# One pool of eight PSUM banks and no root tables in a two-layer kernel; squares on ScalarE; the gate, the weighted sums and the factors of operands on GpSimd

## The chip, the core and the metric

The kernel runs on one core of a Trainium2 chip. The core has a matrix engine (TensorE, PE in the profile; its weight loads are PEld), three engines for elementwise work (VectorE or DVE, ScalarE or ACT, GpSimd or POOL), a queue that issues DMAs (SP), a memory for tiles of 128 partitions (SBUF), and an accumulator memory, PSUM, of eight banks of 128 x 512 float32, which TensorE fills and VectorE and ScalarE read. The metric is the device time of one launch in microseconds (us). Everything is float32.

## The reference

Two transformer layers over x of shape 16 x 512 x 128 (sequences b = 0..15, 512 tokens, width 128), each an attention and a feed-forward part on the same normalised input:

```python
# layer 0
xn = layernorm(x)
q, k = phi(rope(xn @ Wq.T)), phi(rope(xn @ Wk.T))        # 16 heads of 8; phi = elu + 1
num, den = cumulative sums over earlier tokens of k v and of k, applied to q
attn = (num / max(den, 1e-6)) @ Wo.T
p, i = top_k(softmax(xn @ router_w.T), 2)                # of 8 experts
moe = sum over the two: p / sum(p) * square(relu(xn @ w_fc[e].T)) @ w_proj[e].T
x = x + attn + moe + square(relu(xn @ shared_fc.T)) @ shared_proj.T
# layer 1
xn = layernorm(x)
# softmax attention in chunks of 64 queries, each chunk seeing the keys up to its own end;
# each head's probabilities are scaled by a gate computed from their sum (two steps of a small
# dynamical system with tanh, clips and products), then normalised again
attn = out @ W_out.T
mix = sigmoid(xr @ W_r.T) * (square(relu(xk @ W_k.T)) @ W_v.T)   # xr, xk blend xn with the token before
x = x + attn + mix
```

## The kernel before

**Tiling.** A sequence is four tiles of 128 tokens. The 16 sequences go in groups of 3, 4, 4, 3 and 2 (`GROUPS`, L47). For a group, `dispatch` (L1042) normalises x, routes the tokens and scatters them to expert slots in DRAM by indirect DMAs from POOL (`send`, L1091). `slot_tiles` (L1126) goes over the slot tiles four at a time: SP fetches rows and each tile's expert weights, `hidden` (L1168) makes the hidden activations of a pair of tiles (product, relu on ScalarE, square on VectorE or POOL, L1181), `project` (L1184) the second product, and results go back to DRAM. `layer0` runs the linear attention of each sequence (`linear_operands` L831, `linear_attention` L921) and then `shared_expert` (L1010). `layer1` runs for each sequence a `head` (L1526: gather both experts' rows and add them, `combine` L1219; layernorm; `channel_mix` L1451; values; `projected` L1298; `operands` L1307) and a `body` (L1546) of two halves u = 0 and 1, each of eight heads; `tail` (L1482) applies the gate (`gated` L1427, `gate_factor` L1237) and the output product.

**Layer 1's attention.** `operands` first computes score units (sc) for the row maxima: five units for each half, each of 4 x 512 columns in strips of 32 rows, which VectorE reduces (maxima). `weighted` (L1365) computes the scores again with the maxima folded in (st), takes the exponential on ScalarE (ex) and accumulates the products with v into `po` (o1, L1369), which stays open for the whole half. Factors for operands: for u = 0 VectorE makes qa and ka in one instruction each, for u = 1 POOL makes each in two (L1317 to 1322).

**PSUM.** Two pools: `ps_big` with three tiles of two banks and `ps_one` with two tiles of one bank (L509 to 516). Scores (sc, st) take two big tiles for a unit; hg, h, qkv, qk and the transposes of q and k take a big one; all others take one of the two single banks.

**Order.** The program is not written in the order of issue. Generators emit operations with their engine and data needs; `Program.run` (L332) is a planner that walks a simulated clock with a cost for each kind of instruction (`COSTS`, L215; `TURN`, L222, for PE's change between full-height and 32-row or 32-column products) and picks for each engine the earliest operation that is ready; buffers are handed out in simulated time too (`_take`, L414). What it picks becomes the fixed order on each engine. Operations inside `with program.unit()` (L326) stay together on PE. An indirect DMA is "spaced" (L472): it waits for the PE instruction that was emitted last before it (L474), and at least 1.9 us of simulated time lie between two. All engine instructions come out of one helper, so the profile gives them all as L261; groups are told apart by the tiles they write and read. L1095 and L1114 are the indirect DMAs.

**Layernorm** (L649): statistics on VectorE, the root on ScalarE (L657), which shares that engine with exponentials and tanh, reciprocal and normalisation on VectorE.

## Time and profile before

| | |
|---|---|
| median of the runs | 1670.35 us (1669.26 to 1676.13, 3 runs) |
| profiled execution | 1665.29 us, of which the span from first to last instruction 1663.5 us |
| instructions | 36439 |
| mean granted clock of TensorE | 0.973 |
| indirect DMAs on POOL | 128 scatters of 1.06 us, 128 gathers of 1.00 us |
| ACT table loads | 48 of 1.28 us |
| reductions for the maxima | 448, 385.8 us on VectorE |
| DMA | 167.03 MB, 99 GB/s to and from HBM over the span |

A busy PE in the profile is not PE at its peak: the ends of products are modelled, and a product that stands waiting inside a run of products counts as busy. In the table by stage a stretch of the span is a line: its length, the busy time of each engine with the number of instructions, TensorE's granted clock, the share of DMA time. In groups, what follows the first bar is busy us and the mean ns of one instruction; what follows the second is the idle time just before them and who ended it. A line of waits gives the total, how often, and the longest.

### The profile page before, as it was taken

To read this page: it belongs to the slowest core of one execution; us is meant where nothing else is said; L and a number is where in the kernel's file an instruction comes from. 1 tells how busy PE (TensorE), PEld (TensorE's weight loads), DVE (VectorE), ACT (ScalarE), POOL (GpSimd) and SP (SyncE) were. 2 spreads that over 40 slices of the span, in tenths; PEclk is the share of its full clock that TensorE was granted. 3 is DMA by queue.
4 is the path that set the end of the run, shared out by engine and by line. 5 is a ranking of instruction groups with operands and counts; after the bars stand their busy time and mean duration, and the time that the engine had idled before them with its cause. 6 is when DMAs were issued, how large, how long until landed. Compare 5 with 4: busy or idle time off the path is not lost.

```text
span 1663.5 us, 36439 instructions
## 1 busy us (share of the span) xinstructions
PE 1547.3 (93%) x14439; PEld 1021.8 (61%) x14439; DVE 1207.5 (73%) x2474; ACT 778.2 (47%) x1191; POOL 539.1 (32%) x485
## 2 busy tenths in 40 slices
PE   4889799999999999999999989999999999999996
PEld 3578776666766566566666656666565656565443
DVE  7875268877578874976758796968786858786773
ACT  4343334545445634444544655454545444535444
POOL 1415255075125421453033603242136202135020
PEclk8899999999999999999999999999999999999998
DMA  5367777144334423243322243324133313110000
GB/s 155 106 211 233 219 218 212 49 141 118 96 107 127 127 87 96 72 121 97 90 90 79 78 122 96 96 63 124 35 94 92 110 33 86 30 51 23 20 1 14
DMA packets 154986, 167.03 MB, mean 100 GB/s; under 512 B 13248, under 2 KB 100672, under 8 KB 154816
## 3 DMA queue, kind: packets, MB, share of 16 engines
q1 hardware_dynamic: 146624, 147.91, 29.9%
q0 software_dynamic: 8192, 16.79, 3.3%
q8 instruction: 114, 1.87, 0.5%
q14 instruction: 56, 0.46, 0.1%
HBM read 122.83 MB, written 41.81 MB: 99 GB/s over the span
## 4 chain that ended last, share of the span: by engine, by line
PE 53%; DVE 10%; issue 5%; ACT 3%; POOL 1%; DMA 0%; SPq 0%; POOLq 0%; ACTq 0%; DVEq 0%
PE o L261 10%; PE sc L261 10%; PE st L261 8%; PE yg_ps L261 5%; PE hg_ps L261 5%; DVE maxima L261 4%; PE y L261 3%; PE h_ps L261 2%; PE qkv L261 1%; PE qk L261 1%; PE ho_a L261 1%; ACT ex L261 1%; PE oh_a L261 1%; PE mx L261 1%; PE cm_r L261 1%
## 5 line engine op out<-in xcount | busy, mean ns | idle before, releaser
L261 DVE TENSOR_REDUCE maxima<-sc 128x2 f32<-128x768 f32 (+2 forms) x448 | 385.8, 912 | 84.6 <-PE sc L261 83.0
L261 ACT ACTIVATE ex<-st 128x1024 f32<-128x1024 f32 x320 | 313.1, 1025 | 177.5 <-PE st L261 176.3
L261 PE MATMUL st<-qa,ka 32*128 32x384 f32 (+3 forms) x2048 | 213.4, 471 | 9.6 <-DVE maxima L261 5.9
L261 PE MATMUL sc<-ka,qa 32*128 32x512 f32 (+2 forms) x1792 | 213.8, 511 | 3.7 <-DVE maxima L261 1.0
L1095 POOL DMA_INDIRECT rows<-xn,pl_slot x128 | 135.1, 1055 | 225.6 <-PE y L261 64.2
L261 PE MATMUL yg_ps<-wp,hg 128*128 128x128 f32 x1304 | 188.5, 287 | 17.5 <-DVE hg L261 9.4
L261 PEld LDWEIGHTS yg_ps<-wp,hg 128*128 128x128 f32 x1304 | 162.6, 195 | 66.9 <-issue 36.6
L1114 POOL DMA_INDIRECT back<-results,pl_slot x128 | 128.4, 1003 | 222.7 <-PE st L261 38.4
L261 PE MATMUL hg_ps<-xgT,wf 128*128 128x128 f32 x1304 | 182.5, 285 | 10.8 <-issue 6.3
L261 DVE TENSOR_TENSOR am<-sc,const_sb 128x1024 f32<-128x1024 f32 x128 | 151.3, 1218 | 53.7 <-PE sc L261 49.2
L261 PEld LDWEIGHTS hg_ps<-xgT,wf 128*128 128x128 f32 x1304 | 163.5, 196 | 35.9 <-issue 23.8
L261 PE MATMUL o<-ex,vpad 128*32 128x512 f32 (+3 forms) x2048 | 175.1, 447 | 1.7 <-ACT yg L261 1.3
L261 PEld LDWEIGHTS st<-qa,ka 32*128 32x128 f32 x2048 | 104.0, 186 | 81.4 <-issue 26.4
L261 ACT ACTIVATE hg<-hg_ps 128x1024 f32<-128x1024 f32 x84 | 84.2, 1002 | 135.7 <-PE hg_ps L261 135.3
L261 POOL TENSOR_TENSOR hg<-hg 128x1024 f32<-128x1024 f32 x34 | 64.6, 1901 | 224.1 <-ACT hg L261 223.9
L261 PEld LDWEIGHTS sc<-ka,qa 32*128 32x128 f32 x1792 | 90.5, 185 | 70.5 <-issue 25.8
L261 PEld LDWEIGHTS o<-ex,vpad 128*32 128x32 f32 x2048 | 52.2, 110 | 83.8 <-issue 59.5
L261 DVE TENSOR_TENSOR hg<-hg 128x1024 f32<-128x1024 f32 (+1 forms) x50 | 62.0, 1241 | 56.4 <-ACT hg L261 56.4
L261 ACT COPY oTs<-o 128x256 f32<-128x256 f32 (+1 forms) x96 | 42.7, 445 | 120.2 <-PE o L261 119.5
L261 ACT COPY yg<-yg_ps 128x256 f32<-128x256 f32 x84 | 30.9, 368 | 131.6 <-PE yg_ps L261 108.6
L261 PE MATMUL o<-am,vpad 128*32 128x128 f32 x2048 | 81.8, 281 | 8.7 <-DVE am L261 8.0
L261 PE MATMUL sc<-q0m,k0T 32*128 32x256 f32 x1024 | 81.3, 410 | 1.6 <-ACT ex L261 1.0
(193 smaller groups left out, 2289.1 us busy)
## 6 DMA issues: line engine op xcount, KB each, us to landing
wf<-in_w_fc SPq DMA_DIRECT2D x163, 256.0 KB
wp<-in_w_proj SPq DMA_DIRECT2D x163, 256.0 KB
results<-yg SPq DMA_DIRECT2D x79, 128.0 KB
xg<-rows SPq DMA_DIRECT2D x37, 256.0 KB
rows<-zeros SPq DMA_DIRECT2D x2, 2496.0 KB
x_in<-in_x SPq DMA_DIRECT2D x16, 256.0 KB
x<-x SPq DMA_DIRECT2D x16, 256.0 KB
out<-rr SPq DMA_DIRECT2D x16, 256.0 KB
```

What stands on the lines that cost most here:

```text
L261: return getattr(api, method)(*map(made, args), **{k: made(a) for k, a in kw.items()})
L1095: i = nc.gpsimd.indirect_dma_start(out=rows.made()[:, :], out_offset=bass.IndirectOffsetOnAxis(ap=slot.made(), axis=0), in_=row.made(), in ...
L1114: "POOL", lambda: nc.gpsimd.indirect_dma_start(out=o.made(), out_offset=None, in_=results.made()[:, :], in_offset=bass.IndirectOffsetOnAxi ...
```

## The change

- **PSUM**: one tile of eight banks (`Banks`). A tile asks for one bank or for two adjacent ones; the planner picks which, by the earliest time and by how many banks it would leave without their neighbour. hg and h take single banks, one relu each, as do the transposes of q and of k.
- **Root**: POOL adds the epsilon and takes the power -0.5; the Sqrt on ScalarE and VectorE's reciprocal are gone.
- **Squares**: those that VectorE made (hg and h) are a Square on ScalarE; those on POOL stay, and so does channel_mix's.
- **To POOL**: the gate's arithmetic but for reciprocals and fused operations; the weighted sum of expert rows (one product with the share, one add, for all four tiles); the masked copies of q in layer 0 (q0m, before on ScalarE from PSUM); the operands of u = 1 in wider instructions; for the last two sequences (`LATE`) also the operands of u = 0, the normalisation and the gate's factor.
- **To ScalarE**: the two scalings in channel_mix.
- **Units**: the products of a hidden tile, of `project`, of `projected` and of `shared_expert`'s y stay together on PE.
- **Planner**: costs for POOL and for scalar operands of VectorE changed; two small routing tiles share buffers with others.

```diff
+LATE = B - GROUPS[-1]
...
+class Banks:
+    def __init__(self, pool, n, ahead):
+        self.pool, self.n, self.whole = pool, n, None
+        self.slots = Slots(n, ahead)
+        self.slots.free = [(0.0, k) for k in range(n)]
+    def tile(self, shape, name):
+        base = Base(self.slots, lambda: self._made(base))
+        base.psum, base.banks = True, shape[1] if len(shape) == 3 else 1
+        self.slots.asked.append(base)
+        base.turn = len(self.slots.asked) - 1
+        return View(base, shape)
+    def _made(self, base):
+        if self.whole is None:
+            self.whole = self.pool.tile([P, self.n, 512], F32, tag="banks", name="banks")
+        if base.banks == 1:
+            return self.whole[:, base.at[0], :]
+        return self.whole[:, base.at[0] : base.at[0] + base.banks, :]
+    @staticmethod
+    def place(slots, bs, start):
...
-    ("ACT", None): (200, 0.8), ("POOL", None): (120, 1.75), ("SP", None): (80, 0.0),
+    ("ACT", None): (200, 0.8), ("POOL", None): (240, 1.63), ("POOL", "fast"): (120, 1.14),
+    ("POOL", "each"): (60, 2.97), ("POOL", "memset"): (100, 0.84), ("SP", None): (80, 0.0),
 }
+EACH = 75
...
-    ps_big = pool("ps_big", 3, 24, space=bass.MemoryType.PSUM)
-    ps_one = pool("ps_one", 2, 24, space=bass.MemoryType.PSUM)
+    banks = Banks(
+        ctx.enter_context(tc.tile_pool(name="psum", bufs=1, space=bass.MemoryType.PSUM)), 8, 48
+    )
     def big(name):
-        return ps_big.tile([P, 2, 512], F32, tag="big", name=name)
+        return banks.tile([P, 2, 512], name)
     def one(name):
-        return ps_one.tile([P, 512], F32, tag="one", name=name)
+        return banks.tile([P, 512], name)
...
-    eps = fixed.tile([P, 1], F32, tag="eps", name="eps")
-    V.memset(eps, LN_EPS)
+    root = fixed.tile([P, NT], F32, tag="root", name="root")
+    V.memset(root, -0.5)
...
-    def layernorm_T(xs, xT, name, tag, bufs):
+    def layernorm_T(xs, xT, name, tag, bufs, late=False):
...
-        S.activation(rstd, mv[:, :, 1], AF.Sqrt, bias=eps, scale=1.0)
-        V.reciprocal(rstd, rstd)
+        G.tensor_scalar_add(rstd, mv[:, :, 1], LN_EPS)
+        G.tensor_tensor(rstd, rstd, root, ALU.pow)
         xn = p2.tile([P, NT, D], F32, tag=tag, name=f"xn_{name}", bufs=bufs)
         for t in range(NT):
-            V.tensor_scalar(
+            (G if late else V).tensor_scalar(
...
-        pts = big(f"qkT_ps_{b}")
-        for s in range(2):
+        q_tag, k_tag, bufs = home["T"]
+        both = []
+        for s, (tag, n) in enumerate(((q_tag, "q0T"), (k_tag, "k0T"))):
+            pts = one(f"qkT_ps_{b}_{s}")
             for t in range(NT):
                 M.transpose(
-                    pts[:, s, t * P : (t + 1) * P], qr[:, t, s * D : (s + 1) * D], ident
+                    pts[:, t * P : (t + 1) * P], qr[:, t, s * D : (s + 1) * D], ident
                 )
-        q_tag, k_tag, bufs = home["T"]
-        qT = p2.tile([P, T], F32, tag=q_tag, name=f"q0T_{b}", bufs=bufs)
-        S.copy(qT, pts[:, 0, :])
-        kT = p2.tile([P, T], F32, tag=k_tag, name=f"k0T_{b}", bufs=bufs)
-        S.copy(kT, pts[:, 1, :])
+            oT = p2.tile([P, T], F32, tag=tag, name=f"{n}_{b}", bufs=bufs)
+            S.copy(oT, pts)
+            both.append(oT)
+        qT, kT = both
         qms = []
         for u in range(2):
             tag, bufs = home["q0m"]
             qm = (p3 if tag == "probs" else p2).tile(
                 [P, 2, T], F32, tag=tag, name=f"q0m_{b}_{u}", bufs=bufs
             )
-            for o in range(2):
-                r = 2 * u + o
-                S.activation(qm[:, o, :], pts[:, 0, :], AF.Copy, scale=c_("pick")[:, r : r + 1])
+            G.tensor_tensor(
+                qm, qT.unsqueeze(1).to_broadcast([P, 2, T]),
+                c_("pick")[:, 2 * u : 2 * u + 2].unsqueeze(2).to_broadcast([P, 2, T]), ALU.mult,
+            )
...
         for fp in range(2):
-            ph = big(f"h_ps_{b}_{fp}")
+            hf = hs[fp]
             for i in range(2):
                 f = 2 * fp + i
-                M.matmul(
-                    ph[:, i, :], wfc_s[:, f * P : (f + 1) * P], xnT, start=True, stop=True
-                )
-            hf = hs[fp]
-            S.activation(hf, ph, AF.Relu)
-            (V if fp or b < GROUPS[0] else G).tensor_tensor(hf, hf, hf, ALU.mult)
+                ph = one(f"h_ps_{b}_{f}")
+                M.matmul(ph, wfc_s[:, f * P : (f + 1) * P], xnT, start=True, stop=True)
+                S.activation(hf[:, i, :], ph, AF.Relu)
+            if fp or b < GROUPS[0]:
+                S.activation(hf, hf, AF.Square)
+            else:
+                G.tensor_tensor(hf, hf, hf, ALU.mult)
...
+        with program.unit():
+            for t in range(NT):
+                cols = slice(t * P, (t + 1) * P)
+                M.matmul(py[:, t, :], oT[:, cols], w_("wo0"), start=True, stop=False)
...
         def hidden(xgT, ws, q, pair):
-            ph = big(f"hg_ps_{g}_{q}_{pair}")
+            h = p2.tile([P, 2, FF], F32, tag="hid", name=f"hg_{g}_{q}_{pair}", bufs=4)
+            o = h[:, 0 : len(ws), :]
             for ii, (wf, _) in enumerate(ws):
                 i = 2 * pair + ii
-                for f in range(NF):
-                    M.matmul(
-                        ph[:, ii, f * P : (f + 1) * P], wf[:, f * P : (f + 1) * P],
-                        xgT[:, i * P : (i + 1) * P], start=True, stop=True,
-                    )
-            h = p2.tile([P, 2, FF], F32, tag="hid", name=f"hg_{g}_{q}_{pair}", bufs=4)
-            o = h[:, 0 : len(ws), :]
-            S.activation(o, ph[:, 0 : len(ws), :], AF.Relu)
-            (V if pair or g == 0 else G).tensor_tensor(o, o, o, ALU.mult)
+                ph = one(f"hg_ps_{g}_{q}_{i}")
+                with program.unit():
+                    for f in range(NF):
+                        M.matmul(
+                            ph[:, f * P : (f + 1) * P], wf[:, f * P : (f + 1) * P],
+                            xgT[:, i * P : (i + 1) * P], start=True, stop=True,
+                        )
+                S.activation(h[:, ii, :], ph, AF.Relu)
+            if pair or g == 0:
+                S.activation(o, o, AF.Square)
+            else:
+                G.tensor_tensor(o, o, o, ALU.mult)
             return h
         def project(h, ws, n):
             py = one(f"yg_ps_{g}_{n}")
-            for ii, (_, wp) in enumerate(ws):
-                for f in range(NF):
-                    M.matmul(
-                        py[:, ii * P : (ii + 1) * P], h[:, ii, f * P : (f + 1) * P],
-                        wp[:, f, :], start=(f == 0), stop=(f == NF - 1),
-                    )
+            with program.unit():
+                for ii, (_, wp) in enumerate(ws):
+                    for f in range(NF):
+                        M.matmul(
+                            py[:, ii * P : (ii + 1) * P], h[:, ii, f * P : (f + 1) * P],
+                            wp[:, f, :], start=(f == 0), stop=(f == NF - 1),
+                        )
...
-            for t in range(NT):
-                n = k * NT + t
-                V.scalar_tensor_tensor(
-                    x1[:, t, :], y[:, t, :], shares[j][:, n, :], x1[:, t, :],
-                    ALU.mult, ALU.add,
-                )
+            share = shares[j][:, k * NT : (k + 1) * NT, :]
+            G.tensor_tensor(y, y, share.to_broadcast([P, NT, D]), ALU.mult)
+            G.tensor_tensor(x1, x1, y, ALU.add)
...
         n = NT * H
+        A = G
         def new(tag):
             return tiny.tile([P, n], F32, tag=f"gf_{tag}", name=f"gf_{tag}_{b}", bufs=1)
         rl, en, sc, cur, v, w, z, g = (new(x) for x in ("rl", "en", "sc", "cur", "v", "w", "z", "g"))
         V.reciprocal(rl, sums)
-        V.tensor_mul(en, sums, rl)
-        V.tensor_scalar_max(sc, en, 1e-6)
+        A.tensor_mul(en, sums, rl)
+        A.tensor_scalar_max(sc, en, 1e-6)
         V.reciprocal(cur, sc)
-        V.tensor_mul(cur, cur, en)
+        A.tensor_mul(cur, cur, en)
         S.activation(g, en, AF.Tanh, bias=gate_bias, scale=5.0)
-        V.tensor_scalar(g, g, 0.45, 0.55, ALU.mult, ALU.add)
-        V.tensor_mul(cur, cur, g)
...
+        A.tensor_mul(rl, rl, g)
+        A.tensor_mul(rl, rl, z)
...
-        def spread(name, k):
-            a = c_(name)[:, k * HALVES : (k + 1) * HALVES]
-            return a.unsqueeze(2).to_broadcast([P, HALVES, P // 2])
+        def spread(name, k, n):
+            a = c_(name)[:, k * HALVES : (k + n) * HALVES]
+            return a.unsqueeze(2).to_broadcast([P, n * HALVES, P // 2])
         at_ = PAIR if u == 0 else 0
-        def build(o, i, own, aug):
-            if u == 0:
-                V.scalar_tensor_tensor(halves(o), halves(i), own, aug, ALU.mult, ALU.add)
-            else:
-                G.tensor_scalar_mul(o, i, own)
-                G.tensor_tensor(halves(o), halves(o), aug, ALU.add)
+        q, k = qk[:, 0, :], qk[:, 1, :]
+        own = c_("own")[:, u : u + 1]
+        parity = c_("parity")[:, 2 * u : 2 * u + 2]
         qa = p2.tile([P, T], F32, tag="qa", name=f"qa_{b}_{u}")
-        build(qa, qk[:, 0, :], c_("own")[:, u : u + 1], spread("aug_q", u))
         ka = p2.tile([P, 2, T], F32, tag="ka", name=f"ka_{b}_{u}")
-        for k in range(2 * u, 2 * u + 2):
-            build(
-                ka[:, k % 2, :], qk[:, 1, :], c_("parity")[:, k : k + 1], spread("aug_k", k)
+        if u == 0 and b < LATE:
+            V.scalar_tensor_tensor(
+                halves(qa), halves(q), own, spread("aug_q", u, 1), ALU.mult, ALU.add
             )
+            for o in range(2):
+                V.scalar_tensor_tensor(
+                    halves(ka[:, o, :]), halves(k), parity[:, o : o + 1],
+                    spread("aug_k", 2 * u + o, 1), ALU.mult, ALU.add,
+                )
+        else:
+            G.tensor_tensor(qa, q, own.to_broadcast([P, T]), ALU.mult)
+            G.tensor_tensor(halves(qa), halves(qa), spread("aug_q", u, 1), ALU.add)
+            G.tensor_tensor(
+                ka, k.unsqueeze(1).to_broadcast([P, 2, T]),
+                parity.unsqueeze(2).to_broadcast([P, 2, T]), ALU.mult,
+            )
+            ka_ = ka.rearrange("p o t -> p (o t)")
+            G.tensor_tensor(halves(ka_), halves(ka_), spread("aug_k", 2 * u, 2), ALU.add)
...
-        V.tensor_tensor(ov, ov, fac.unsqueeze(2).to_broadcast([P, NT * H, DH]), ALU.mult)
+        (G if b >= LATE else V).tensor_tensor(ov, ov, fac.unsqueeze(2).to_broadcast([P, NT * H, DH]), ALU.mult)
...
-            V.tensor_scalar_mul(m, xp[:, 0:T], om)
+            S.activation(m, xp[:, 0:T], AF.Copy, scale=om)
...
-        yield from layernorm_T(x1, xp[:, 1 : T + 1], f"1_{b}", "xn1", 1)
+        yield from layernorm_T(x1, xp[:, 1 : T + 1], f"1_{b}", "xn1", 1, b >= LATE)
```

## The prediction

> **What bounds the kernel.** I read, in this order: busy time by engine, a table by stage, the timeline of two stretches, TensorE's waits, the groups. First, the engines:
>
> ```profile
> PE 1547.3 (93%) x14439; PEld 1021.8 (61%) x14439; DVE 1207.5 (73%) x2474; ACT 778.2 (47%) x1191; POOL 539.1 (32%) x485
> ```
>
> TensorE (PE) looks like the bound, with 1663.5 - 1547.3 = 116 us idle. The busy figure hides more. Timeline near the end (start, duration, engine, group):
>
> ```profile
> 1594.12 1.14 PE L261 MATMUL sc<-ka,qa 32*128 32x512 f32 x8
> ...
> 1600.88 7.16 DVE L261 TENSOR_REDUCE maxima<-sc 128x2 f32<-128x768 f32 x10
> ...
> 1601.44 6.65 PE L261 MATMUL sc<-ka,qa 32*128 32x384 f32 x32
> ```
>
> One score unit (all of it 2048 result columns in four strips) takes 1.14 us. The last line is two units, so 2.3 us of work "busy" for 6.65 us: PE sits inside a unit until VectorE (DVE) has reduced a PSUM tile and freed it. Over the whole span the groups give 213.8 + 81.3 us for 224 units of sc (1.32 each) and 213.4 us for 160 of st (1.33): 0.19 us above 1.14, times 384 units, is **73 us of stall hidden in "busy"**. Stages, with busy us of PE, PEld, DVE, ACT, POOL, then clock, DMA share, GB/s:
>
> ```profile
> 0.00:40.00 40.00, 19.29 (x72) 12.46 (x73) 29.44 (x116) 17.73 (x34) 7.97 (x24) 0.90 0.53 161
> 160.00:240.00 80.00, 70.40 (x599) 63.86 (x597) 31.91 (x54) 28.18 (x45) 32.95 (x29) 0.95 0.69 211
> 240.00:280.00 40.00, 37.25 (x287) 27.57 (x287) 39.27 (x87) 15.43 (x27) 23.51 (x20) 0.96 0.62 189
> 520.00:560.00 40.00, 40.00 (x416) 25.20 (x408) 35.69 (x96) 27.66 (x38) 17.42 (x18) 1.00 0.31 96
> 560.00:600.00 40.00, 34.89 (x262) 23.31 (x257) 35.43 (x73) 20.74 (x35) 18.71 (x17) 0.91 0.51 149
> 960.00:1000.00 40.00, 34.98 (x279) 21.95 (x281) 37.72 (x81) 20.28 (x31) 4.85 (x3) 1.00 0.36 104
> ```
>
> A good stretch keeps PE full. Where it falls to 35, DVE stands at 35 to 39 of 40: there DVE sets the pace. At 160 to 240 (experts of group 0) DVE is idle more than half, and PE waits on latency. The mean clock of 0.973 is worth 0.027 x 1663.5 = 45 us; the first two slices of 40 us (0.90, 0.84) and the last (0.72 over 23.5) hold 17 of it, the rest follows idle stretches in the body. So PE is the bound, with some 190 us of stall and 28 us of clock around it. PE's waits (total, times, longest):
>
> ```profile
> PE y L261 <- ACT oT_a L261: 1.3, 2, 0.7
> ...
> PE o L261 <- ACT yg L261: 1.3, 1, 1.3
> ```
>
> Both are a product waiting for the evacuation of an unrelated tile: both tiles live in the two single banks (L515), and o1 (L1369) keeps one of these for a whole half of an attention. Such lines add to about **20 us**.
>
> **The change, part by part.** Groups that price it (busy, mean ns, idle before):
>
> ```profile
> L261 POOL TENSOR_TENSOR hg<-hg 128x1024 f32<-128x1024 f32 x34 | 64.6, 1901 | 224.1 <-ACT hg L261 223.9
> ...
> L261 DVE TENSOR_TENSOR hg<-hg 128x1024 f32<-128x1024 f32 (+1 forms) x50 | 62.0, 1241 | 56.4 <-ACT hg L261 56.4
> ...
> L261 ACT ACT_TABLE_LOAD x48 | 61.6, 1283 | 21.2 <-PE st L261 19.2 <-PEq L1699 0.7 <-DVE phi L261 0.6
> ...
> L261 DVE SCALAR_TENSOR_TENSOR x<-back,rt_m,x 128x128 f32<-128x128 f32 x128 | 45.1, 404 | 10.6 <-DMA back<-results,pl_slot 10.6
> ```
>
> *DVE* loses the squares (62.0 + 23.0 us), 20 small operations of the gate for each of 16 batches (their rows add to 80.1), the weighted sums (45.1), the scaling in channel_mix (9.4 + 7.7), the reciprocal of layernorm (5.4), and for the last two batches some 10 (operands 4.9, normalising 3.9, factor 1.4): **-243 us, to about 965**. The 386 us of maxima stay.
>
> *ScalarE* gains 69 squares at 1.02 us (ex, the same 128x1024, has 1025 ns; +71), 84 + 32 relus as two of 0.60 instead of one of 1.02 (+19), 32 scalings at 0.71 (q0m, a copy with a scale per partition, has 713 ns; +23); it loses 47 of 48 table loads (-60), q0m (39.4 busy), roots (-10): +4 in all, hidden under its 885 us of idle. Here a rule weighs otherwise. The row: 1.28 us for a load, 21.2 us of idle before all 48. The Trainium skill (ScalarE: Activation LUTs, "What ACT_TABLE_LOAD costs") adds a drain of about 1.38, so the loads would be worth 47 x 2.66 = 125 us. The row shows at most 0.44 us before each, so I take 60; by the rule ScalarE would end 65 us lower and the sum below would move only where it waits for ScalarE at the start, by perhaps 5.
>
> *GpSimd (POOL)* takes the gate: 11 two-tensor operations of 64 columns (1901 at 1024 and 1059 at 512 columns give 217 + 1.64 n, so 0.32 us) and 9 with a scalar (0.18 to 0.3): 5.4 us for a batch, against 5.0 on DVE, **+87**; the sums, 32 x 2 x 1.06 = +68; q0m, 32 x 1.90 = +61; operands of the second half as 1.06 + 1.06 + 1.90 + 1.90 = 6 us instead of 8, -32; late work +19; the root's add and power, unseen: between 0.2 (two of the shortest, memset 0.105) and 2.1 us (two as long as an indirect DMA's 1.05); I take 0.6, near the small operations, +19. Together **539 to about 760**. The second rule speaks against this. The skill (SBUF — State Buffer, "Who interferes with whom") says that DVE instructions with two SBUF inputs or in a two-port mode share a port pair with GpSimd under an exclusive lock. The trace has it:
>
> ```profile
> 962.92 1.89 POOL L261 TENSOR_TENSOR h<-h 128x1024 f32<-128x1024 f32 x1 [11.77 <-ACT h L261]
> 974.36 1.89 POOL L261 TENSOR_TENSOR hg<-hg 128x1024 f32<-128x1024 f32 x1 [9.54 <-ACT hg L261]
> ```
>
> and DVE's 64-column gf_z at 974.40 lasts 1.94 us, not 0.23. Summed over DVE's instructions against their own undisturbed time the loss is 55 us. GpSimd's arithmetic grows from about 265 to 490 us, by which the rule alone would make it 102. But DVE's instructions of that kind (squares 85, gate 80, normalising 48, sums 45, rotation and phi 74, operands 39, mixing 44, others 15) fall from about 430 us to 200, so 55 x 1.85 x 0.465 = 47: no worse. By the rule alone DVE would gain 55 us less, and the sum some 10 less.
>
> *Waits that it adds.* The sum of a batch waits in POOL's queue for four gathers to land; behind it stand the next gathers and scatters, each tied to a position of PE (L474), and behind those q0m (awaited by the scores of layer 0), the gate and the second half's operands. q0m is ready at 0.59 + 3.8 us after the transposes instead of 0.59 + 0.60 + 2.44, +0.8 us, hidden by the other chains' products (DVE and PE of layer 1). SP gets no new DMA, but a store of x1 or out comes later with its sum. If the cover goes, 0.8 x 16 = 13 us.
>
> *PSUM.* One pool lets hg and h take single banks freed one by one, and leaves the pairs to the scores.
>
> *The sum*, with the ends of what can't be seen:
> - score units: 73 us of stall, 0 (the reductions alone pace it) to 73; a third, since reductions stay: 24
> - PE idle in slices where DVE is full (240, 560, 680, 960, 1040, 1280: 21 us): half, 10
> - single banks: 20 us, half, 10
> - experts of group 0: 9.6 us idle, half; the square follows two relus of which one overlaps products: 5
> - start: five table loads of 1.28 lie between roots and exponentials there; 4 of 6.4
> - changes of form: of 410 stretches of full-height work, 91 hold only a projection, only a y or only an hg; units bring some together: 50 x 0.15 us (L222 reckons 138 to 208 ns) = 8, between 0 and 20
> - clock: 6 of 28
> - against it: the last batch's gate, alone at the end (8.3 us of PE idle), on two engines with some ten handovers: -3; both halves' operands of the last batch in one queue: -2; lateness in POOL's queue, 0.4 us for a batch: -6 (0 to 25).
>
> 67 - 11 = 56. The profiled execution took 1665.3 us, so 1609; the median shown is 5 above it: **1614 us** (3.4% less).
>
> **Rivals.**
> *PE's order is the bound* and stays so: reductions pace the scores, idle DVE time goes nowhere. For it: PE is full at 520 to 560 with DVE at 35.7. Then only start and single banks: 14 - 11, so **1667**, the change not doing what it says. Against it: the slices where DVE is full.
> *The score stalls go altogether*: the 49 us not counted, and a little clock: **1560**. Against it: ten reductions at 0.72 us each in the 7.16 above.
> *GpSimd's queue becomes the bound*, the slower one. Each batch hands over there four times (gather and sum, q0m, gate, operands); gathers wait for PE and block the rest. For it: POOL waits up to 20.4 us at a gather for PE. Against it: POOL idles 1124 us. Decisive at 56/16 = 3.5 us for a batch uncovered; at 5.5 us the loss is 88: +32, **1702**.
>
> **How the numbers follow.** Forecast 0.56 (its own range 1590 to 1640), PE's order 0.10, all stalls gone 0.14, queue 0.20. Under 0.5% a measurement can't tell a change from none (1662 to 1679). Faster: 0.56 + 0.14 + half of the second = 0.75; same 0.05; slower 0.20. The range leaves out half of the third case below and about half of the queue's above: 1565 to 1690.
>
> **What would show it.** DVE near 965 us and no slice above 36 of 40; one table load; POOL near 760; sc and st near 1.25 us for a unit; fewer waits for unrelated evacuations; the gap before the last oh_a at 10 to 11 us. I am wrong if sc and st stay at 1.32, or if PE waits for POOL (q0m, ka, xn) by more than some 20 us in all; a square that needs its own table would show as loads again.

## The result, and the profile after

The changed kernel takes **1727.1 us** (median of 4 runs, 1721.1 to 1733.1) where the kernel before took 1672.7 beside it: ratio **1.0325**, 95% interval 1.028 to 1.037. It is slower by 54 us; the forecast was 1614, and its range ended at 1690. The profiled execution took 1721.1 us, its span is 1718.7.

The engines' sums came out roughly as reckoned. Busy time of the changed kernel, and from its groups the one table load that is left:

```profile
PE 1524.8 (89%) x14439; PEld 1011.4 (59%) x14439; DVE 1023.7 (60%) x1877; ACT 783.6 (46%) x1260; POOL 796.6 (46%) x951
```
```profile
L317 ACT ACT_TABLE_LOAD x1 | 1.3, 1283 | 0.7 <-PEq L1791 0.7
```

VectorE (DVE) lost 184 us, ScalarE gained 5, GpSimd (POOL) gained 258. TensorE (PE) is busy 22 us less, but its idle time went from 116 to 194 us, and its granted clock from 0.973 to 0.960: one minus the clock, times the span, is 45 us before and 69 after. Where PE waits (total, times, longest), first in the kernel before, then in the changed one, where every PSUM tile is called banks:

```profile
PE ln_ps L261 <- DVE xn L261: 11.4, 2, 9.4
...
PE oh_a L261 <- DVE o1n L261: 8.3, 1, 8.3
...
PE st L261 <- DVE maxima L261: 5.9, 11, 1.5
```

```profile
PE banks L317 <- DVE maxima L317: 39.5, 43, 5.4
PE banks L317 <- DVE xn L317: 28.2, 6, 9.3
...
PE banks L317 <- POOL o1n L317: 11.3, 1, 11.3
...
PE banks L317 <- POOL hg L317: 9.5, 5, 3.5
...
PE banks L317 <- POOL xk L317: 5.8, 5, 2.7
...
PE banks L317 <- POOL q0m L317: 2.0, 2, 1.1
...
PE banks L317 <- POOL xn L317: 1.3, 3, 0.4
```

All such lines together, PE's waits for VectorE went from 74 to 109 us, those for ScalarE from 22 to 44, those for GpSimd itself from under 1 to 30. The largest growth of single kinds is in the waits for VectorE's reductions (10.5 to 39.5, all tiles together) and for normalised rows (11.4 to 28.2). The score units as groups (busy, mean ns of one, idle before), before and then after:

```profile
L261 PE MATMUL st<-qa,ka 32*128 32x384 f32 (+3 forms) x2048 | 213.4, 471 | 9.6 <-DVE maxima L261 5.9
L261 PE MATMUL sc<-ka,qa 32*128 32x512 f32 (+2 forms) x1792 | 213.8, 511 | 3.7 <-DVE maxima L261 1.0
...
L261 PE MATMUL sc<-q0m,k0T 32*128 32x256 f32 x1024 | 81.3, 410 | 1.6 <-ACT ex L261 1.0
```
```profile
L317 PE MATMUL banks<-ka,qa 32*128 32x512 f32 (+2 forms) x1792 | 195.7, 517 | 33.3 <-DVE maxima L317 15.9
L317 PE MATMUL banks<-qa,ka 32*128 32x512 f32 (+3 forms) x2048 | 197.9, 473 | 18.7 <-DVE maxima L317 10.6
...
L317 PE MATMUL banks<-q0m,k0T 32*128 32x256 f32 x1024 | 79.7, 419 | 8.3 <-DVE maxima L317 5.8
```

A unit of sc takes (195.7 + 79.7) / 224 = 1.23 us, one of st 1.24, as forecast. But the stall only stepped out of the unit and stands in front of it: busy and idle together were 508.5 + 14.9 = 523 us before and are 473.3 + 60.3 = 534 now. Three stretches of 40 us (columns as in the table by stage of before):

```profile
240.00:280.00 40.00, 29.16 (x194) 22.87 (x194) 18.29 (x43) 10.92 (x18) 24.54 (x25) 0.83 0.40 121
...
560.00:600.00 40.00, 30.79 (x306) 19.28 (x304) 23.02 (x63) 16.46 (x24) 25.39 (x27) 0.83 0.38 112
...
960.00:1000.00 40.00, 35.41 (x353) 22.18 (x345) 29.23 (x56) 19.36 (x31) 31.05 (x33) 0.96 0.37 107
```

PE is far from full although VectorE stands at only 18 to 29 of 40. All three lie where the expert results of a group of batches are gathered. The whole stretch of gathers of the second group, of before and then of after:

```profile
499.00:602.00 103.00, 96.89 (x895) 62.57 (x897) 88.70 (x210) 57.70 (x84) 48.57 (x46) 0.97 0.39 115
```
```profile
528.00:654.00 126.00, 109.96 (x990) 73.09 (x992) 78.36 (x147) 54.63 (x88) 85.75 (x95) 0.93 0.40 119
```

GpSimd is busy 68% of it instead of 47%, and that leaves out what it waits; over the whole span it is 46%. Its queue there (start, duration, and in brackets the idle time before and its releaser):

```profile
544.36 1.04 POOL L1193 DMA_INDIRECT back<-results,pl_slot  x1 [1.90 <-PE banks L317]
545.42 0.33 POOL L317 TENSOR_TENSOR gf_rl<-gf_rl,gf_z 128x64 f32<-128x64 f32 x1
547.13 1.04 POOL L317 TENSOR_TENSOR back<-back,rt_m 128x512 f32<-128x512 f32 x1 [1.37 <-DMA back<-results,pl_slot]
548.25 1.27 POOL L317 TENSOR_TENSOR x<-x,back 128x512 f32<-128x512 f32 x1
549.67 0.99 POOL L1193 DMA_INDIRECT back<-results,pl_slot  x1
550.96 0.94 POOL L1193 DMA_INDIRECT back<-results,pl_slot  x1 [0.31 <-issue]
552.83 0.94 POOL L1193 DMA_INDIRECT back<-results,pl_slot  x1 [0.93 <-PE banks L317]
554.08 0.94 POOL L1193 DMA_INDIRECT back<-results,pl_slot  x1 [0.30 <-issue]
558.94 1.04 POOL L317 TENSOR_TENSOR back<-back,rt_m 128x512 f32<-128x512 f32 x1 [3.92 <-DMA back<-results,pl_slot]
560.06 1.26 POOL L317 TENSOR_TENSOR x<-x,back 128x512 f32<-128x512 f32 x1
561.47 0.99 POOL L1193 DMA_INDIRECT back<-results,pl_slot  x1
```

Four gathers, then the product, which stands 3.92 us until the last gather has landed, then the addition, and only then the next gather. In the kernel before, the gathers run on while VectorE adds beside them (lines between these are left out):

```profile
508.31 0.95 POOL L1114 DMA_INDIRECT back<-results,pl_slot  x1 [1.11 <-PE hg_ps L261]
...
509.58 1.13 DVE L261 SCALAR_TENSOR_TENSOR x<-back,rt_m,x 128x128 f32<-128x128 f32 x4
...
510.25 1.02 POOL L1114 DMA_INDIRECT back<-results,pl_slot  x1 [1.00 <-PE hg_ps L261]
...
512.39 0.94 POOL L1114 DMA_INDIRECT back<-results,pl_slot  x1 [1.11 <-PE hg_ps L261]
```

### The profile page after: what moved, and what is told of

The parts are those of the page before. It is cut to its first block, busy times and chain, and to the rows that moved or that the text cites. A ratio compares the mean times of both kernels' runs of the same rounds, so it can differ in the third digit from the quotient of the medians.

```text
span 1718.7 us, 36520 instructions
## 1 busy us (share of the span) xinstructions
PE 1524.8 (89%) x14439; PEld 1011.4 (59%) x14439; DVE 1023.7 (60%) x1877; ACT 783.6 (46%) x1260; POOL 796.6 (46%) x951
## 4 chain that ended last, share of the span: by engine, by line
PE 64%; DVE 15%; POOL 8%; issue 5%; DMA 4%; ACT 4%; POOLq 0%; SPq 0%; DVEq 0%; ACTq 0%
PE banks L317 64%; DVE maxima L317 5%; DMA back<-results,pl_slot 3%; POOL back L1193 1%; ACT ex L317 1%; DVE am L317 1%; POOL back L317 1%; DVE xn L317 1%; ACT hg L317 1%; POOL ln_rstd L317 1%; DVE qr L317 1%; POOL gf_z L317 1%; DVE pl_ef L317 1%; POOL x L317 1%; POOL rows L1174 1%
## 5 line engine op out<-in xcount | busy, mean ns | idle before, releaser
L317 DVE TENSOR_REDUCE maxima<-banks 128x2 f32<-128x768 f32 (+2 forms) x448 | 384.5, 911 | 127.2 <-PE banks L317 123.8
L317 ACT ACTIVATE ex<-banks 128x1024 f32<-128x1024 f32 x320 | 312.4, 1024 | 169.5 <-PE banks L317 163.4
L317 PE MATMUL banks<-ka,qa 32*128 32x512 f32 (+2 forms) x1792 | 195.7, 517 | 33.3 <-DVE maxima L317 15.9
L317 PE MATMUL banks<-qa,ka 32*128 32x512 f32 (+3 forms) x2048 | 197.9, 473 | 18.7 <-DVE maxima L317 10.6
L317 DVE TENSOR_TENSOR am<-banks,const_sb 128x1024 f32<-128x1024 f32 x128 | 150.6, 1216 | 102.4 <-PE banks L317 78.2
L317 PEld LDWEIGHTS banks<-xgT,wf 128*128 128x128 f32 x1304 | 160.3, 193 | 42.6 <-issue 19.7
L317 PE MATMUL banks<-xgT,wf 128*128 128x128 f32 x1304 | 179.2, 283 | 5.6 <-DVE maxima L317 2.4
L317 PE MATMUL banks<-wp,hg 128*128 128x128 f32 x1304 | 166.4, 282 | 18.3 <-POOL hg L317 9.5
L317 PE MATMUL banks<-ex,vpad 128*32 128x512 f32 (+3 forms) x2048 | 176.9, 446 | 0.9 <-ACT ex L317 0.8
L317 PEld LDWEIGHTS banks<-wp,hg 128*128 128x128 f32 x1304 | 155.9, 195 | 34.0 <-issue 11.1
L317 POOL TENSOR_TENSOR q0m<-q0T,const_sb 128x1024 f32<-128x1024 f32 x32 | 60.3, 1899 | 59.9 <-ACT q0T L317 54.2
L317 PE MATMUL banks<-q0m,k0T 32*128 32x256 f32 x1024 | 79.7, 419 | 8.3 <-DVE maxima L317 5.8
```

The lines of the kernel that those rows point to most:

```text
L317: return getattr(api, method)(*map(made, args), **{k: made(a) for k, a in kw.items()})
```

## The experiments

Two questions: is it the PSUM part or the moves to GpSimd, and which move, by what. A point of ratio below is 16.7 us; intervals are 95%. Runs are compared by their ratios to the kernel before, each measured beside it. A difference of two such ratios is uncertain by 5 to 9 us, and one of a few us says little.

**1. All moves undone, or the pool alone.** The first run puts gate, sums, root, q0m, operands and late work back on the engines they came from (the diffs of 3 and 8). The second has of the change only the class of banks, its placement, and this:

```diff
-    ps_big = pool("ps_big", 3, 24, space=bass.MemoryType.PSUM)
-    ps_one = pool("ps_one", 2, 24, space=bass.MemoryType.PSUM)
+    banks = Banks(ctx.enter_context(tc.tile_pool(name="psum", bufs=1, space=...)), 8, 48)
```

> The changed kernel with everything that went to GpSimd put back where it was (gate, weighted sums, root of layer 1, q0m, operands, late work); the one PSUM pool, the units, the halved relus, the squares and the mixing on ScalarE stay. Theory A (GpSimd's in-order queue is late and hands its lateness to TensorE): the loss goes and what the PSUM part brings shows, 1620 to 1665 us, GpSimd busy 500 to 560, VectorE about 1130. Theory B (the one pool and its placement, or the order that comes with it, cost the time): it stays at 1700 to 1735, with TensorE's waits for the maxima still near 40 us.

> The kernel before with the one pool of eight banks and its placement alone; all operations, engines and costs as before. Theory A: 1645 to 1675 us, faster or the same, score units at 1.25 us instead of 1.32. Theory B: slower than 1690, waits of TensorE for maxima about 40 us instead of under 10.

Measured: moves undone 1637.4 us, **0.9811** (0.978 to 0.984); the pool alone 1712.2 us, **1.0272** (1.025 to 1.029). So theory A holds for the changed kernel: without the moves it beats the kernel before by 31 us. And B holds of the pool by itself: with pairs for the hidden layers it costs 45 us. The score units are 487.6 us busy with 64.0 idle in front of them, together 28 us more than before; the other 17 were not traced.

**2. The PSUM part alone** (pool, hidden layers and transposes in single banks with a relu for each, units; squares and all engines as before). Beside the pool's lines above, for the experts (for h likewise):

```diff
-            ph = big(f"hg_ps_{g}_{q}_{pair}")
             for ii, (wf, _) in enumerate(ws):
+                ph = one(f"hg_ps_{g}_{q}_{i}")
+                with program.unit():
                     for f in range(NF):
                         M.matmul(ph[...], ...)
-            S.activation(o, ph[:, 0 : len(ws), :], AF.Relu)
+                S.activation(h[:, ii, :], ph, AF.Relu)
             (V if pair or g == 0 else G).tensor_tensor(o, o, o, ALU.mult)
```

> The kernel before with all that the change does to PSUM and TensorE's order (one pool of eight banks, hidden layers and transposes in single banks with a relu for each, units) and nothing else: squares, gate, sums, q0m, roots as before. Theory C (halves and units are what makes the one pool pay; with pairs it fragments): 1640 to 1665 us. Theory D (the one pool loses in any form, and the squares on ScalarE won what the run with the moves undone won): 1690 to 1715, like the pool alone.

Measured: 1664.7 us, **0.9927** (0.991 to 0.995), score units 463.6 + 48.6 = 512 us. Theory C: single banks and units together are worth 3.5 points on top of the pool; which of the two brings it was not separated. The rest to 0.9811, 1.2 points or 19 us, is the squares and the mixing on ScalarE, and with them the planner's new costs, which alone do next to nothing (0.9978, 0.996 to 0.9995):

```diff
-    ("ACT", None): (200, 0.8), ("POOL", None): (120, 1.75), ("SP", None): (80, 0.0),
+    ("ACT", None): (200, 0.8), ("POOL", None): (240, 1.63), ("POOL", "fast"): (120, 1.14),
+    ("POOL", "each"): (60, 2.97), ("POOL", "memset"): (100, 0.84), ("SP", None): (80, 0.0),
```

> The kernel before with the changed kernel's planner costs for VectorE and GpSimd alone (the charge for a root kept): every instruction the same, only the planned order moves. It shows how far an order alone moves the time. If order is a small matter: 1655 to 1680. If a new order by itself costs what the pool alone did: 1690 or more.

**3. Gate or sums back, from the changed kernel.**

```diff
-        A = G
+        A = V
```
```diff
-            G.tensor_tensor(y, y, share.to_broadcast([P, NT, D]), ALU.mult)
-            G.tensor_tensor(x1, x1, y, ALU.add)
+            for t in range(NT):
+                V.scalar_tensor_tensor(x1[:, t, :], y[:, t, :], shares[j][:, n, :], x1[:, t, :],
+                    ALU.mult, ALU.add)
```

> The changed kernel with the 20 gate operations of a batch back on VectorE. GpSimd loses some 87 us of work, VectorE gains 80. Theory A, in equal parts by GpSimd's work (87 of 258 us added): 1727 - 0.34 x 112 = 1690, range 1675 to 1705, with the layernorm's and the weighted sums' waits shorter. Theory B: 1715 to 1735.

> The changed kernel with the weighted sums of expert rows back on VectorE, one instruction per 128 tokens. GpSimd loses 75 us of work and 56 us in which its queue stood at a gather that had not landed. Theory A, where it is the waiting in the queue that counts: 1680 to 1695 us. Theory B: 1715 to 1735.

Measured: gate back 1719.8 us, 1.0294 (1.025 to 1.034), no difference that can be told; sums back 1661.4 us, **0.9959** (0.994 to 0.998). The sums alone carry 3.7 points, 61 us, more than was expected. They are no more than 75 of the 258 us of work that GpSimd gained, so it isn't the amount of work alone. Where the two kernels part shows when both are read at equal progress (the matmuls done, each weighted with the planner's cost):

```
stretch of the changed kernel, us      lag behind "sums back" grows by, us
   0 -  238                              -1.9
 238 -  450   gathers from  226          16.9
 450 -  508                              -0.5
 508 -  648   gathers from  528          11.9
 648 -  889                               0.7
 889 - 1090   gathers from  909          17.1
1090 - 1277                              -0.5
1277 - 1410   gathers from 1272           6.7
1410 - 1542                               0.7
1542 - 1714   gathers from 1517           4.4
```

All of it is lost in the stretches that open with a group's gathers, none in the others. The gathers themselves end at 315, 654, 1029, 1342 and 1561; in the first stretch about half of the loss comes after them.

**4. The sums alone, in the kernel before** (the second diff of 3, the other way round).

> The kernel before with the weighted sums of expert rows on GpSimd and nothing else changed. Theory A (the sum waits for the gather at the head of GpSimd's queue): slower by 30 to 65 us, 1695 to 1730, gathers of groups 1 and 2 3.5 to 4 us apart instead of 3.2 and 2.4. Theory E (the sums cost only together with the gate and q0m in the same queue): 1660 to 1680.

Measured: 1719.0 us, **1.0237** (1.021 to 1.027). GpSimd waits for gathers to land:

```profile
POOL back L261 <- DMA back<-results,pl_slot: 75.6, 30, 5.1
```

Theory A: 40 us are lost with no gate and no q0m in the queue. A rival would be that the new work on GpSimd makes VectorE's own instructions last longer. Counted over those that took more than 0.1 us above the tenth percentile of their group, the lengthening is 58 us in the kernel before and 52 here, so this is not how the sums cost their time.

**5. All eight gathers ahead of both sums.**

```diff
+        ys = []
         for j in range(2):
             y = p2.tile([P, NT, D], F32, tag="back", ...)
             for t in range(NT):
                 fetch(y[:, t, :], ...)
+            ys.append(y)
+        yield
+        for j, y in enumerate(ys):
             share = shares[j][:, k * NT : (k + 1) * NT, :]
             G.tensor_tensor(y, y, share.to_broadcast([P, NT, D]), ALU.mult)
```

> The changed kernel with all eight gathers of a batch issued ahead of both of its weighted sums, which stay on GpSimd; the same instructions in another order. In the changed kernel's trace each half of a batch goes four gathers, a wait for the last to land (0.4 to 3.9 us, 56 us in 27 waits), product, addition, and only then the next four gathers. Theory A1 (that standing wait costs the time): about half of the waits go, 1685 to 1710 us, and the gathers of groups 1 and 2 come closer than 3.9 and 3.8 us apart. Theory A2 (what counts is GpSimd's work in the chain, 2.3 us for a half instead of 1.6, and the engine's load): the same as the changed kernel, 1715 to 1735.

Measured: 1748.4 us, **1.0421** (1.040 to 1.044), slower still, against both. A1 fell as it was put: the waits for a landing did not become fewer but more (69.3 us in 29). Why does a planner that keeps times put a sum there? Its line on when a follower may start answers: the time until a DMA has landed (later) counts only where the follower sits on another engine. For VectorE's sums that was so; for a sum on GpSimd the data count as there when the gather has been issued.

**6. The landing counted.**

```diff
-                seen = end + (op.later if other.engine != name or name == "SP" else 0.0) + ...
+                seen = end + (op.later if other.engine != name or name == "SP" or op.spaced else 0.0) + ...
```

> The changed kernel with one line of its planner changed: the time in which an indirect gather lands also counts for an instruction of GpSimd's own queue (until now it counted only for other engines, so a sum on GpSimd was planned straight behind its own gather). Same instructions, same engines. Theory A3 (the sum stands at the head of the queue because the planner takes its data to be there, and the next gathers stand behind it): GpSimd's waits for a gather fall from 56 us to below 20, the batches of a group follow one another at about 20 us instead of 25 to 38, and 30 to 55 us come back, 1670 to 1695. Theory A2 (GpSimd's longer sums and its load are what cost): 1715 to 1735 as before.

Measured: 1705.3 us, **1.0218** (1.020 to 1.024). GpSimd's waits for gathers, in the changed kernel and then here:

```profile
POOL back L317 <- DMA back<-results,pl_slot: 56.3, 27, 3.9
```
```profile
POOL back L317 <- DMA back<-results,pl_slot: 20.8, 12, 5.4
```

Three gathers of the next half now go ahead of the product:

```profile
543.22 0.99 POOL L1193 DMA_INDIRECT back<-results,pl_slot  x1 [0.16 <-issue]
544.58 0.95 POOL L1193 DMA_INDIRECT back<-results,pl_slot  x1 [0.37 <-PE banks L317]
548.14 0.95 POOL L1193 DMA_INDIRECT back<-results,pl_slot  x1 [2.62 <-PE banks L317]
549.21 1.04 POOL L317 TENSOR_TENSOR back<-back,rt_m 128x512 f32<-128x512 f32 x1
550.33 1.27 POOL L317 TENSOR_TENSOR x<-x,back 128x512 f32<-128x512 f32 x1
```

The mechanism of A3 is there, at 1.1 points (18 us), a third of what the sums cost; its 30 to 55 us were too much. Some 43 us stayed open.

**7. What else in the sums.** From the changed kernel, the same two instructions on VectorE; and from the run with the moves undone, the two on GpSimd as the only move, with the landing counted.

```diff
-            G.tensor_tensor(y, y, share.to_broadcast([P, NT, D]), ALU.mult)
-            G.tensor_tensor(x1, x1, y, ALU.add)
+            V.tensor_tensor(y, y, share.to_broadcast([P, NT, D]), ALU.mult)
+            V.tensor_tensor(x1, x1, y, ALU.add)
```

> The changed kernel with each weighted sum as the same two whole-batch instructions (product, addition), but on VectorE. If the engine and its queue cost the time and not the form: like the run with the sums back, 1650 to 1675. If two coarse instructions in the place of four (x ready for the layernorm only as a whole, longer on the way) carry it: 1695 or more.

> The run with the moves undone (0.981), with the sums alone on GpSimd and the landing of a gather counted in the plan; gate, root, q0m and operands are off GpSimd. Theory A2' (what is left of the sums' cost is GpSimd's queue being full in the stretches with gathers: gathers, squares, mixing, gate, q0m and sums one behind another): with the queue emptied of the rest the sums cost under 12 us, 1630 to 1650. Theory A4 (the sums on GpSimd cost by themselves, since half of x waits for a queue in which gathers are tied to TensorE's positions): 1660 to 1685.

Measured: on VectorE 1678.7 us, 1.0066 (1.004 to 1.009): of 3.7 points, 1.1 are the coarser form (18 us) and 2.6 the engine with its queue (43 us). Alone and counted 1650.2 us, **0.9884** (0.985 to 0.992), only 0.7 points or 12 us above the run without them, at the upper end of what A2' gave. So with landing counted the sums cost 12 us beside no other move and 2.6 points, 43 us, beside all of them (run 6 against the sums back).

**8. The other moves, one at a time**, each added to the run with the moves undone (0.9811). The edits, as they stand in that run and in the changed kernel (the late work is the constant LATE, B in that run; the operands' form is in the diff of the change):

```diff
-        A = V
+        A = G
...
-        S.activation(rstd, mv[:, :, 1], AF.Sqrt, bias=eps, scale=1.0)
-        V.reciprocal(rstd, rstd)
+        G.tensor_scalar_add(rstd, mv[:, :, 1], LN_EPS)
+        G.tensor_tensor(rstd, rstd, root, ALU.pow)
...
-            for o in range(2):
-                S.activation(qm[:, o, :], qT, AF.Copy, scale=c_("pick")[:, 2*u+o : 2*u+o+1])
+            G.tensor_tensor(qm, qT.unsqueeze(1).to_broadcast([P, 2, T]), ..., ALU.mult)
```

> The run with the moves undone (0.981 of the time before), with the gate alone on GpSimd. VectorE 80 us less, GpSimd 87 us more. As the prediction had it (VectorE's relief counts where it is full): 1615 to 1632. If the gate's handovers between GpSimd, VectorE and ScalarE cost as much as the relief gives: 1632 to 1645. If it carries the 24 us between that run and the one with the sums alone back: 1655 to 1665.

> The run with the moves undone, with the root alone as an addition and a power on GpSimd (0.25 + 1.04 us) and one table load instead of 48. As the prediction had it (table loads hidden, start 4 us earlier): 1628 to 1640. If the normalised rows come late through GpSimd's queue (TensorE's waits for xn 14 us in that run, 28 in the changed kernel): 1645 to 1660.

> The run with the moves undone, with q0m alone on GpSimd (3.8 us a batch in two instructions). If q0m in the queue behind gathers tied to TensorE carries the loss of the operands' run (1.0056 against 0.981, 40 us): 1655 to 1675. If other chains hide it, as the prediction had it: 1630 to 1642.

> The run with the moves undone, with the last two batches' operands, normalising and gate factor alone on GpSimd. As the prediction had it: 1632 to 1645. If this late work carries the loss of the operands' run: 1650 to 1670, all of it after 1450 us of the span.

> The run with the moves undone, with q0m on GpSimd, the operands of layer 1 in four two-tensor instructions and the last two batches' operands, normalising and factor on GpSimd. As the prediction had it (q0m hidden by other chains, late work +2): 1630 to 1645. If the operands' and the late work's queue carries the 24 us: 1650 to 1662, with the tail after the last sums 10 us or more longer.

The root's run also drops the planner's charge of 2600 ns for a Sqrt.

| moved alone | ratio (interval) | against 0.9811 |
|---|---|---|
| gate | 0.9943 (0.992 to 0.997) | +22 us |
| root | 0.9763 (0.974 to 0.979) | -8 us |
| q0m | 1.0028 (1.001 to 1.005) | +36 us |
| late work | 0.9842 (0.981 to 0.987) | +5 us |
| q0m, late work, operands together | 1.0056 (1.004 to 1.008) | +41 us |

The operands' new form is thus worth nothing that can be told (41 - 36 - 5, uncertain by 9). The late work lies in the range that the prediction gave it, and its 5 us can't be told from none. The expectation for q0m ("other chains hide it") did not come out, and the three together are slower than both expected ranges. The parts don't add: summed they would put "sums back" at 1.014, and it is 0.9959.

The gate shows what such a move does to the engine that is to be relieved. VectorE's waits for GpSimd in the run with the gate moved:

```profile
DVE gf_z L317 <- POOL gf_z L317: 49.9, 24, 5.0
DVE gf_v L317 <- POOL gf_z L317: 15.2, 13, 2.0
DVE gf_cur L317 <- POOL gf_sc L317: 13.7, 13, 2.5
DVE o1n L317 <- POOL gf_rl L317: 10.6, 8, 3.2
```

Five of a batch's gate operations stayed on VectorE between those on GpSimd. It got rid of 77 us of work (1110.5 to 1033.7) and stands idle 89 us before these operations; with the gate on VectorE such waits are 2.8 us.

For q0m, PE waits 0.5 us in the run that loses 36. What shows instead, at equal progress against the run without it: 9 us lost by 170 us, 10 more in and just after the second group's gathers, 15 in the third's; and VectorE's instructions last 70 us longer than undisturbed instead of 48 (counted as in 4). As much, 24 us of lengthening, lies in instructions that run beside q0m's own on GpSimd. Whether the place in the queue or these collisions carry the 36 was not separated.

**9. The queue's fullness, tested forward.** First the changed kernel with the landing counted and q0m back; then the run with the root moved, with the squares that were still on GpSimd moved to ScalarE (the same for the experts' squares):

```diff
-            if fp or b < GROUPS[0]:
-                S.activation(hf, hf, AF.Square)
-            else:
-                G.tensor_tensor(hf, hf, hf, ALU.mult)
+            S.activation(hf, hf, AF.Square)
```

> The changed kernel with the landing of a gather counted in the plan (1.022 of the time before) and q0m back on ScalarE; sums, gate, root and operands stay on GpSimd. Theory A2' (the sums cost because GpSimd's queue is full in the stretches with gathers): q0m's 3.8 us a batch out of it bring 20 to 40 us, 1665 to 1685. If q0m cost what it did only at the start and by itself: 1690 to 1710.

> The run with the root alone moved (0.976 of the time before, the fastest so far), with the first squares of each pair too on ScalarE, so that GpSimd squares nothing (50 instructions of 1.9 us, 95 us off its queue; ScalarE 51 us more). If work off GpSimd's queue is worth time wherever it stands near gathers: 1605 to 1622. If these squares were off the path and ScalarE's queue takes the loss: 1625 to 1645.

Measured: 1672.2 us, **0.9986** (0.997 to 1.000), 2.3 points or 39 us better with q0m back, inside what A2' gave. But q0m cost as much by itself (36 us, run of 8, without the sums), so this run does not show that q0m makes the sums dearer. And 1624.0 us, **0.9694** (0.967 to 0.972), the fastest of all, 50 us under the kernel before beside it (1674.3) and so faster than both kernels; against the run with the root alone it gains 0.7 points, or 11 us for 95 us of work taken off GpSimd, just short of the 1605 to 1622 expected. Its busy times, and the stretch of the second group's gathers:

```profile
PE 1490.2 (92%) x14439; PEld 998.9 (62%) x14439; DVE 1075.4 (66%) x2341; ACT 862.3 (53%) x1371; POOL 478.7 (29%) x502
```
```profile
497.00:597.00 100.00, 96.24 (x947) 64.94 (x945) 84.75 (x207) 59.88 (x97) 49.79 (x54) 1.00 0.44 130
```

PE is 96% busy there at full clock, and VectorE's lengthening is down to 19 us. For the sums A2' rests on the 12 and 43 us of 7: what they cost depends on the other moves beside them, and the loss falls where the gathers are. Which of these moves it is, and whether by their place in the queue, is not shown.

## Why the prediction was wrong

The step that failed is **"lateness in POOL's queue, 0.4 us for a batch: -6 (0 to 25)"**. The prediction named the place (a sum waits in POOL's queue for gathers to land, behind it the next gathers, q0m and the gate) and mis-sized the term. The sums cost 61 us, 3.8 us a batch. Of these, 18 are the coarser form, which the prediction put at nothing; 43, or 2.7 us a batch, are GpSimd with its queue, seven times the 6 and beyond the 25. Planning the landing takes back 18. How the rest comes about is open beyond this: with the landing planned and no other move on GpSimd, the sums cost 12.

A second step failed with it: q0m, "hidden by the other chains' products" and at most 13 us if that cover went, cost 36 to 39. By which path is open.

Of the 113 us between 1614 and 1727, the sums hold 55 (61 less the 6 reckoned). The sums-back kernel, at 1661, still stands 47 above the forecast, so other terms failed too.

What happened is nearest to the third rival, which decided at "3.5 us for a batch uncovered" and gave 1702. It had 0.20, since "POOL idles 1124 us" stood against it: a mean over the span, where the queue's room counts in the stretches with gathers. There GpSimd went from 47% to 68% busy, with its waits on top.

Step by step:
- **Score units** (24). The unit's time came out, the gain did not. In the changed kernel the stall moved in front (523 to 534 us in all); with the moves undone it was 514, in the fastest run 494.9. The term assumed that a stall that leaves a unit leaves the kernel.
- **Single banks and forms** (10 and 8). With the score units 42 together; the PSUM part alone brought 12. The pool by itself cost 45, which no case held.
- **Slices where DVE is full** (10). The squares and the mixing, with the planner's costs, brought about 19, but the gate cost 22 alone instead of helping (in the changed kernel 5 or nothing): the step counted VectorE's busy time and not its place in a chain of handovers.
- **Start and root** (4). 8, somewhat better or the same, though the power takes 1.04 us, so that both instructions take 1.3 and not 0.6.
- **Last batch**: the gate's +3 came out (PE's wait for the last o1n 11.3 instead of 8.3 us), the late work's +2 measured 5, uncertain by as much.
- **Clock** (6). 24 us were lost instead (45 to 69).
- **Collisions** (47 us). 76 in the changed kernel (counted as in 4; before 58), 29 more, which is part of why VectorE is at 1024 and not 965. The estimate scaled with busy times over the span; the runs gave 19 to 95 us and don't follow these (36 with the gate alone moved, 48 without it; 95 in the changed kernel with the gate back on VectorE, which may be why that brought nothing).
- **What would show it wrong**: "PE waits for POOL (q0m, ka, xn) by more than some 20 us" was the wrong sign. These lines hold 2.0 + 1.3 us; with o1n, hg and xk, which it did not name, PE's waits for GpSimd are 30. More reaches PE by way of VectorE, whose lines grew by 35 us, as waits for normalised rows (11.4 to 28.2) and for maxima (10.5 to 39.5, while the stall inside the units shrank).

## What to carry to other kernels

Before an operation is moved to an idle engine, look at that engine in the stretch where the operation falls, with its waits, and ask what stands behind it: a consumer in the same in-order queue as its own DMA holds everything behind it until the data have landed. A planner that reckons with such queues must charge the landing also to a follower on the same engine; here one condition was worth 18 us. Be wary of cutting a chain into pieces on two engines: the gate's saved VectorE 77 us of work, made it wait 89 us and cost 22. Moving a whole chain was not tested.

## What the runs showed of the hardware that was not expected

- A power on GpSimd takes 1.04 us on 128x4 elements, four times an addition of the same shape:

```profile
L317 POOL TENSOR_TENSOR ln_rstd<-ln_rstd,root 128x4 f32<-128x4 f32 x32 | 33.4, 1044 | 2.6
...
L317 POOL TENSOR_SCALAR ln_rstd<-ln_mv 128x4 f32<-128x4 f32 x32 | 8.2, 257 | 45.0 <-DVE ln_mv L317 36.8 <-DVE rda L317 7.3 <-DVE den L317 0.4
```

- The same whole-batch product or addition (128x512) takes 745 ns on VectorE and 1046 or 1285 ns on GpSimd.
- Of the 76 us by which VectorE's instructions were lengthened in the changed kernel, 75 are in instructions that overlap an arithmetic instruction on GpSimd. How much there is does not go by GpSimd's busy time: 95 us with GpSimd busy 692 us (gate back), 76 with 797, 52 with 616 (sums alone), 19 with 479.
- The granted clock is lower in most of the slower runs: 0.945 at a span of 1749 us, 0.960 at 1719, 0.973 at 1637, 0.977 at 1623. One minus the clock, times the span, is 96 us in the first and 37 in the last: 59 of the 126 us between them. But the span alone does not settle it: 0.970 at 1714 (the pool alone), and 0.964 at 1663 (sums back) where the kernel before has 0.973. That stalls cause it was not tested.
